# Attention and a ternary feed-forward layer on one core: Wo centred on chip, the variance behind Wo from ScalarE's sums of squares

## The chip, the cores and the metric

The kernel runs on one core of a Trainium2 chip. The metric is the device time of one execution in microseconds (us), as the median of several runs. The engines are named as the profile names them: PE is TensorE's matrix multiplication and PEld its loading of weights, DVE is VectorE, ACT is ScalarE, POOL is GpSimd, and SP is the engine that issues the DMAs. L818 is line 818 of the kernel before.

## The reference

The input x has 8 sequences of 1,024 tokens of width 256, in f32. Two sublayers follow one another, each with a LayerNorm (without weights) in front and one behind:

```python
x = x + _layernorm(attn(_layernorm(x), Wq, Wk, Wv, Wo))
x = x + _layernorm(ffn(_layernorm(x), weight, alpha, bias))
```

`attn` has 16 query heads of width 16 and 4 key and value heads, with a rotary embedding on queries and keys, a softmax over all 1,024 keys, and the product with Wo (256 x 256) at its end. `ffn` is one product with the ternary form (-1, 0, 1) of a 256 x 256 weight, times alpha, plus bias. `_layernorm` takes off the mean of the 256 elements and divides by the root of the variance plus 1e-5. What matters here is the LayerNorm behind Wo: its input is a = o @ Wo, and the first residual sum is x1 = x + layernorm(a).

## The kernel before

**Tiling.** The 8,192 tokens are cut into 16 units of 512 tokens, two to a sequence. For each unit a *project* part makes normalised tokens, queries, keys and values; 32 *steps* of attention follow (4 groups of heads by 8 blocks of 128 keys); then a *tail* divides by the softmax's sums, multiplies by Wo, and does everything up to the output. A tail has two *pairs* of two token tiles each (a tile is 128 tokens on the partitions by 256). The last tail (`LastTail`) has four parts of one tile each.

**A step.** TensorE computes scores twice: `sm` (L600), from which VectorE takes the row maxima (`mx`, L625), for a block of work ahead of time; and `se` (L673) with the maximum already taken off through extra rows of the queries, of which ScalarE makes the exponentials `e` (L694), 128x512 each. The product with the values, `av` (L714), follows two windows behind; a window is two or three of the four `se` of a step. TensorE's queue alternates `se` and `sm`. PSUM holds three banks in a ring for `se` and for most other products (pools `ps_e`, tag "se"), two double banks for `sm` (`ps_mx`), and one for `av`. A product in the ring waits until ScalarE has read the one three places before it.

**The order.** The instruction order on PE, DVE and ACT is written out by hand in program order, all through; POOL's order, outside the start and the end, and SP's order are chosen by a scheduler at build time. The lists `P_PARTS` and `T_PARTS` say in which of a unit's steps each part of a project and of a tail is issued; the tail of unit u runs beside the attention of unit u + 1 and the project of a later unit. `P_SECOND`, `T_FIRST`, `W_PARTS` and `T_LAST` shift these steps at the start and in the tails of units 12 to 14.

**The tail around Wo.** `attn(p)` multiplies by Wo into `pa` (L301, three products of high and low halves) and copies it to `a` on ScalarE (L818), at step 12 for pair 0 and step 15 for pair 1. `stats_a(p)`, at steps 15 and 17, runs `ln_stats`: on VectorE two BATCH_NORM_STATS2 (`bnst`, L237) and two aggregates (`mv`, L239); on GpSimd three small instructions (L241 to L243) that give minus the mean and 1 / sqrt(variance + eps). `add(p)` then normalises on GpSimd (L253, one instruction per tile, add and multiply) into `x1` and adds the residual `xr` (L823). `stats_x(p)`, from step 19, is the next LayerNorm, with VectorE's statistics of `x1`. The final LayerNorm (`stats_f`) is like it.

**Wo itself** is prepared once, in step 9 (`prepare_wo`): eight DMAs (L960) bring it in, and GpSimd splits it into a high part `woh` (L157) and a low part `wol` (L162).

Other names in the prediction: `xt` and `pt_xt` are transposed activations (L271, L267), `pkv` and `pq` the products for keys with values and for queries (L301), `kv_t` and `q_rot` their copies (L376, L457), `avsb` the copy of a finished `av` (L727), `d_k`, `k_rot` and `t2k` the way of the keys through DRAM and their rotation, `ml` the low part of the maxima that a DMA writes into the queries' extra rows `q_st` (L664), `part` a sum for the ternary threshold (L203).

Of the kernel before, what the change touches and what calls it, by code (L numbers as in the profile page):

```python
# [8 lines left out]
F32 = mybir.dt.float32  # L9
F32R = mybir.dt.float32r  # L10
AF = mybir.ActivationFunctionType
ALU = mybir.AluOpType
AX = mybir.AxisListType
# [3 lines left out]
P = 128  # L17
# [6 lines left out]
EPS = 1e-5  # L24
# [4 lines left out]
def kernel(  # L29
# [29 lines left out]
    nc = tc.nc  # L59
    B, S, D = x.shape  # L60
# [3 lines left out]
    ND = D // P  # L64
# [10 lines left out]
    small = ctx.enter_context(tc.tile_pool(name="small", bufs=4))  # L75
    work = ctx.enter_context(tc.tile_pool(name="work", bufs=2))
# [9 lines left out]
    def load_x(u, tag, bufs):  # L86
        b, half = divmod(u, UPB)
        t = xp.tile([P, UT, D], F32, tag=tag, name=f"{tag}_{u}", bufs=bufs)
        src = x[b, half * UQ : (half + 1) * UQ, :].rearrange("(t p) d -> p t d", p=P)
        for ts in (slice(0, 2), slice(2, 4)) if u == 0 else (slice(0, 4),):  # L90
            nc.sync.dma_start(out=t[:, ts, :], in_=src[:, ts, :])
        return t
# [6 lines left out]
    mhalf = const.tile([P, 2], F32, name="mhalf")  # L99
# [64 lines left out]
    def split(eng, hi, lo, src, hi_eng=None):  # L164

        split_hi(hi_eng or eng, hi, src)
        split_lo(eng, lo, src, hi)


    def parts_of(w, name):  # L170
        return [const.tile(list(w.shape), F32R, name=name + l) for l in "hl"]
# [11 lines left out]
    def psum(shape, name, dtype=F32):  # L183
        if spare[0]:
            spare[0] += 1
            if spare[0] % 5 < 2:
                return ps_mx.tile(shape, dtype, tag="sm", name=name)
        return ps_e.tile(shape, dtype, tag="se", name=name)
# [42 lines left out]
    def ln_stats(src):  # L231

        n = src.shape[1]
        mv = small.tile([P, 2, 2], F32, tag="mv", name="mv")[:, :n]
        st = small.tile([P, 2, 6], F32, tag="bnst", name="bnst")
        for t in range(n):
            nc.vector.bn_stats(st[:, t, :], src[:, t, :])  # L237
        for t in range(n):
            nc.vector.bn_aggr(mv[:, t, :], st[:, t, :])  # L239
        sc = small.tile([P, 2, 2], F32, tag="lnsc", name="lnsc")[:, :, :n]  # L240
        nc.gpsimd.tensor_scalar(sc[:, 1, :], mv[:, :, 1], EPS, 1.0, ALU.add, ALU.mult)  # L241
        nc.gpsimd.tensor_tensor(sc[:, 1, :], sc[:, 1, :], mhalf[:, :n], ALU.pow)  # L242
        nc.gpsimd.tensor_scalar(sc[:, 0, :], mv[:, :, 0], -1.0, 0.0, ALU.mult, ALU.add)  # L243
        return mv, sc
# [52 lines left out]
    def product(out, left, right, terms=TERMS):  # L297

        steps = [(i, j, c) for i, j in terms for c in range(ND)]
        for k, (i, j, c) in enumerate(steps):  # L300
            nc.tensor.matmul(  # L301
                out,
                chunk(left[i], c),
                chunk(right[j], c),
                start=(k == 0),
                stop=(k == len(steps) - 1),
            )
# [15 lines left out]
    class Project:  # L323
# [3 lines left out]
        def __init__(self, u, eng):  # L327
            self.u, self.eng = u, eng
            self.b, self.half = divmod(u, UPB)
            self.xt, self.sc, self.hl = {}, {}, {}  # L330
            self.q_rot = None
            if u not in (1, 2):
                xn = qkp.tile([P, UT, D], F32, tag="xn", name=f"xn_{u}", bufs=2)
                xs = qkp.tile([P, 2, UT, D], F32R, tag="hl", name=f"xs_{u}")
                self.xn = [xn[:, 2 * p : 2 * p + 2, :] for p in range(2)]
                self.xs = [[xs[:, l, 2 * p : 2 * p + 2, :] for l in range(2)] for p in range(2)]
            else:
                self.xn = [
                    tailp.tile([P, 2, D], F32, tag=f"xn{p}", name=f"xn_{u}_{p}") for p in range(2)
                ]  # L340
                self.xs = [
                    [ep.tile([P, 2, D], F32R, tag="e", name=f"xs_{u}_{p}_{l}") for l in range(2)]
                    for p in range(2)
                ]
# [393 lines left out]
    class Tail:  # L738
# [4 lines left out]
        def __init__(self, u):  # L743
            self.u = u
            self.xr = load_x(u, "xr", 1)
            self.a, self.on, self.hl, self.xt, self.x1, self.sc = {}, {}, {}, {}, {}, {}

        def new(self, what, p):
            shape, dtype = ([P, 2, 2, D], F32R) if what == "hl" else ([P, 2, D], F32)
            return tailp.tile(shape, dtype, tag=f"{what}{p}", name=f"{what}_{self.u}_{p}")  # L750
# [62 lines left out]
        def attn(self, p):  # L813
            pa = psum([P, self.width, D], f"pa_{self.u}_{p}")
            for t in range(self.width):
                product(pa[:, t, :], self.heads(self.width * p + t), wo_s)
            self.a[p] = self.new("a", p)
            self.copy(p)(self.a[p], pa)  # L818

        def add(self, p):  # L820
            x1 = self.x1[p] = self.new("x1", p)
# [5 lines left out]
            ln_apply(self.eng(p), self.on[p], self.x1[p], self.sc[p])  # L827

        def stats_a(self, p):
            self.sc[p] = ln_stats(self.a[p])  # L830
            self.add(p)

# [123 lines left out]
    def prepare_wo():  # L956
        wo = tailp.tile([P, ND, D], F32, tag="xn1", name="wo")
        rows = w_o.rearrange("(r c h d) n -> h r d c n", r=HKV, c=2, h=2)
        for i in range(2 * HKV):
            nc.sync.dma_start(out=wo[HD * i : HD * (i + 1)], in_=rows[i // HKV, i % HKV])  # L960
        wo_s.extend(parts_of(wo, "wo"))
        split(nc.gpsimd, *wo_s, wo)

# [97 lines left out]
    for u in range(3, NU):  # L1061
        start = SPU * (u - 4)
        steps = P_FIRST if u == 3 else P_SECOND if u == 4 else [k for k, *_ in P_PARTS]
        at(start + steps[0] - 6, load, u)
        if u == 3:
            for k, stage in (
                (7, measure), (9, prepare_wo), (11, add_up), (13, threshold), (15, ternarize),
                (22, transpose_ternary),
            ):
                at(k, stage)  # L1070
        at(start + steps[0] - 1, begin_project, u)
        for k, (_, *p) in zip(steps, P_PARTS):
            behind = [behind_latest] if u > 4 and p[0] in ("kt", "q_to_dram") else []
            at(start + k, *behind, part, projects, u, *p)
# [254 lines left out]
```

## Time and profile before

| What | Value |
|---|---|
| median of 3 runs | 1624.39 us (1623.93 to 1625.12) |
| span of the profiled execution | 1625.2 us |
| granted TensorE clock, mean | 0.997 |
| PE busy | 1576.5 us, 97% |
| PEld busy | 813.9 us, 50% |
| DVE busy | 1397.1 us, 86% |
| ACT busy | 1270.1 us, 78% |
| POOL busy | 833.8 us, 51% |
| `bnst` of `a` (both LayerNorms that read `a`), DVE | 120 instructions, mean 413 ns |
| `mv` (all LayerNorms), DVE | 256 instructions, mean 174 ns |
| `a<-pa` copy, ACT | 30 instructions, mean 585 ns |
| `e`, ACT | 1,996 instructions, mean 603 ns |

The span runs from the first to the last instruction of one execution, taken by the hardware profiler; the median is of runs timed from outside, and here lies 0.8 us below that span. In the profile's lines the first time is the start in us from the beginning of the span, the second the time for which the group was busy; a number in brackets is how long the engine stood idle just before, and the name behind the arrow is what it then waited for. The *chain of work that ended last* is found by going back from the last instruction, at each step to what released it; its shares say which engine's work the time consists of. The ends of matrix products are modelled, so a busy PE need not be a PE at its peak.

### The profile page before, as it was taken

The numbers are of one execution on the slowest core, as the hardware profiler recorded it, in microseconds if no ns is written. First come the engines' busy times: TensorE is split into PE (matmuls) and PEld (weight loads), VectorE is DVE, ScalarE is ACT, GpSimd is POOL, SyncE is SP. The second block draws the span as 40 slices with busy tenths as digits, with TensorE's granted clock in tenths as the row PEclk, the third lists the DMA queues.
The fourth block names the chain that finished last, engine by engine and source line by source line (L and its number), as shares of the span: only waits on it lengthen the run. The fifth ranks groups of instructions, "written<-read, shape, count | busy, mean of one in ns | idle before, by whom it ended". The sixth has DMA issues, their size and how long they took to land.

```text
span 1625.2 us, 37184 instructions
## 1 busy us (share of the span) xinstructions
PE 1576.5 (97%) x14702; PEld 813.9 (50%) x14702; DVE 1397.1 (86%) x2046; ACT 1270.1 (78%) x2473; POOL 833.8 (51%) x1239
## 2 busy tenths in 40 slices
PE   8999999999999999999999999999999999999997
PEld 6544454454545545454554545455454554444444
DVE  7878888889898888989889898988989888999964
ACT  4667878778787887878788787887878787787774
POOL 5542365364744637455364845546474552333354
PEclk9999999999999999999999999999999999999999
DMA  4151525124151422514133151513314141131100
GB/s 140 53 88 46 113 70 96 57 77 99 57 109 47 102 63 59 120 57 97 59 83 77 57 128 39 105 54 83 79 57 97 46 107 45 42 75 34 43 15 27
DMA packets 86078, 117.98 MB, mean 73 GB/s; under 512 B 12088, under 2 KB 50808, under 8 KB 85752
## 3 DMA queue, kind: packets, MB, share of 16 engines
q1 hardware_dynamic: 85904, 115.60, 29.7%
q8 instruction: 116, 1.90, 0.5%
q14 instruction: 58, 0.48, 0.1%
HBM read 68.65 MB, written 45.88 MB: 70 GB/s over the span
## 4 chain that ended last, share of the span: by engine, by line
PE 81%; DVE 10%; POOL 3%; ACT 2%; issue 2%; DMA 1%; SPq 0%; POOLq 0%; ACTq 0%; DVEq 0%
PE av L714 29%; PE se L673 28%; PE sm L600 9%; DVE mx L625 8%; PE pa L301 3%; PE pq L301 3%; PE pf L301 2%; ACT e L694 2%; PE pt_xt L267 2%; PE pt_ot L267 1%; PE pkv L301 1%; PE pm L648 1%; DVE bnst L237 1%; POOL lnsc L242 0%; DMA x<-in_L_attn_x 0%
## 5 line engine op out<-in xcount | busy, mean ns | idle before, releaser
L625 DVE TENSOR_REDUCE mx<-sm 128x2 f32<-128x1024 f32 (+1 forms) x1301 | 1204.8, 975 | 183.6 <-PE sm L600 164.0
L694 ACT ACTIVATE e<-se 128x512 f32<-128x512 f32 x1996 | 1057.0, 603 | 220.9 <-PE sm L600 163.7
L600 PE MATMUL sm<-k_st,q_st 64*128 64x512 f32 x2048 | 746.5, 448 | 7.2 <-DVE mx L625 4.1
L673 PE MATMUL se<-q_st,k_st 64*128 64x512 f32 x2048 | 705.6, 441 | 18.4 <-ACT e L694 14.6
L714 PE MATMUL av<-e,v_aug 128*32 128x256 f32 (+3 forms) x8584 | 606.0, 378 | 0.0
L673 PEld LDWEIGHTS se<-q_st,k_st 64*128 64x128 f32 x2048 | 324.5, 184 | 396.6 <-ACT e L694 305.4
L600 PEld LDWEIGHTS sm<-k_st,q_st 64*128 64x128 f32 x2048 | 325.2, 184 | 66.4 <-DVE mx L625 44.9
L714 PEld LDWEIGHTS av<-e,v_aug 128*32 128x32 f32 x8584 | 193.5, 108 | 212.5 <-issue 148.9
L241 POOL TENSOR_SCALAR lnsc<-mv 128x2 f32<-128x2 f32 (+1 forms) x134 | 26.1, 195 | 333.1 <-DVE mv L239 326.6
L788 POOL TENSOR_TENSOR xn<-xn,a 128x512 f32<-128x512 f32 x30 | 38.4, 1282 | 135.3 <-DMA a<-d_rec 130.0
L242 POOL TENSOR_TENSOR lnsc<-lnsc,mhalf 128x2 f32<-128x2 f32 (+1 forms) x134 | 92.5, 690 | 0.9
L157 POOL TENSOR_SCALAR xs<-xn 128x512 fp32r<-128x512 f32 x27 | 16.8, 621 | 130.8 <-DMA dq<-hlq 129.5
L162 POOL TENSOR_TENSOR hl<-xn,hl 128x512 fp32r<-128x512 f32 x54 | 68.7, 1285 | 0.1
L253 POOL TENSOR_SCALAR xn<-x,lnsc 128x256 f32<-128x256 f32 x116 | 64.3, 562 | 2.3
L853 POOL TENSOR_TENSOR a<-a,bias_bc 128x512 f32<-128x512 f32 x30 | 38.4, 1279 | 51.9 <-ACT a L852 51.9
L301 PE MATMUL pa<-woh,hl 128*128 128x256 f32 x240 | 46.2, 294 | 1.1 <-ACT e L694 1.1
L237 DVE BATCH_NORM_STATS2 bnst<-x 128x6 f32<-128x256 f32 x124 | 46.0, 413 | 1.3 <-DMA x<-in_L_attn_x 1.3
L315 POOL TENSOR_TENSOR t<-q_rot,sin_q_sb 128x512 f32<-128x512 f32 x31 | 39.7, 1282 | 12.2 <-ACT q_rot L457 12.1
L237 DVE BATCH_NORM_STATS2 bnst<-a 128x6 f32<-128x256 f32 x120 | 44.5, 413 | 0.0
L301 PE MATMUL pq<-xt,wqkvh 128*128 128x256 f32 x256 | 44.1, 294 | 0.5 <-ACT e L694 0.5
L457 ACT COPY q_rot<-pq 128x512 f32<-128x512 f32 x32 | 18.7, 586 | 28.3 <-PE pq L301 28.3
L301 PEld LDWEIGHTS pa<-woh,hl 128*128 128x128 f32 x240 | 34.6, 189 | 12.1 <-issue 6.3
(164 smaller groups left out, 1333.0 us busy)
## 6 DMA issues: line engine op xcount, KB each, us to landing
q_st<-dq SPq DMA_DIRECT2D x90, 256.0 KB
dq<-hlq SPq DMA_DIRECT2D x60, 256.0 KB
d_av<-avsb SPq DMA_DIRECT2D x60, 256.0 KB
x<-in_L_attn_x SPq DMA_DIRECT2D x15, 512.0 KB
xn<-d_av SPq DMA_DIRECT2D x30, 256.0 KB
a<-d_rec SPq DMA_DIRECT2D x30, 256.0 KB
xr<-in_L_attn_x SPq DMA_DIRECT2D x15, 512.0 KB
out_x<-a SPq DMA_DIRECT2D x30, 256.0 KB
```

Source lines behind the costliest of these rows:

```text
L162: eng.tensor_tensor(lo, src, hi.bitcast(F32), ALU.subtract)
L237: nc.vector.bn_stats(st[:, t, :], src[:, t, :])
L242: nc.gpsimd.tensor_tensor(sc[:, 1, :], sc[:, 1, :], mhalf[:, :n], ALU.pow)
L253: eng.tensor_scalar(dst[:, t, :], src[:, t, :], sc[:, 0, t : t + 1] if eng is nc.gpsimd else mv[:, t, 0:1], sc[:, 1, t : t + 1], ALU.add i ...
L267: nc.tensor.transpose(pt[:, c, t * P : (t + 1) * P], src[:, t, c * P : (c + 1) * P], ident_r)
L301: nc.tensor.matmul(out, chunk(left[i], c), chunk(right[j], c), start=(k == 0), stop=(k == len(steps) - 1),)
L315: eng.tensor_tensor(dst, x, table.unsqueeze(1).to_broadcast(list(x.shape)), ALU.mult)
L600: scores = nc.tensor.matmul(sm[0][:, part, :], queries[rows], k_st[(u // UPB) % 3][rows, r2, ch * 512 : (ch + 1) * 512], start=True, stop= ...
L625: early[0] = nc.vector.tensor_reduce(mx[i][:, a, head_and_tile(i, r2, t), lo:n], sm[0][:, lo:n, :], AX.X, ALU.max).ins
L673: nc.tensor.matmul(sc if len(queries.shape) == 2 else sc.rearrange("p (j t) -> p j t", j=G), k_st[(i // G // UPB) % 3][rows, r2, kt * P : ...
L694: nc.scalar.activation(e, sc, AF.Exp, scale=1.0 / D**0.5)
L714: nc.tensor.matmul(av_ps[0][32 * r : 32 * r + 32, lo:hi], va[:, kt, r, :], es[i * NK + kt, r // 2, r % 2][:, lo:hi], start=(kt == 0 and lo ...
```

## The change

Wo's rows are centred once: for each row of Wo its mean over the 256 columns is taken off, by one reduction on VectorE and three instructions on GpSimd. The mean of a row of a = o @ Wo is then zero, so that the variance is the mean of the squares. In all tails but the last, `attn` therefore adds two ScalarE instructions behind the copy of `pa`: Square over each tile, whose output goes to a scratch tile and whose row sum goes to `sq`. `stats_a` no longer calls `ln_stats` there but `add_scaled`: on GpSimd it turns `sq` into 1 / sqrt(sq / 256 + eps) with two small instructions, multiplies each tile by it (one instruction per tile, as before), and adds `xr`. The last tail keeps its statistics. The instructions of the other two LayerNorms stay as they were.

```diff
@@ class Tail, __init__
             self.a, self.on, self.hl, self.xt, self.x1, self.sc = {}, {}, {}, {}, {}, {}
+            self.sq = {}
@@ class Tail, attn
-            self.a[p] = self.new("a", p)
-            self.copy(p)(self.a[p], pa)
+            a = self.a[p] = self.new("a", p)
+            self.copy(p)(a, pa)
+            if self.width == 1:
+                return
+            sq = self.sq[p] = small.tile([P, 2], F32, tag="sq", name=f"sq_{self.u}_{p}")
+            junk = work.tile([P, D], F32, tag="sqj", name=f"sqj_{self.u}_{p}", bufs=1)
+            for t in range(self.width):
+                nc.scalar.activation(junk, a[:, t, :], AF.Square, accum_out=sq[:, t : t + 1])
+
+        def add_scaled(self, p):
+            x1, sq = self.new("x1", p), self.sq[p]
+            nc.gpsimd.tensor_scalar(sq, sq, 1.0 / D, EPS, ALU.mult, ALU.add)
+            nc.gpsimd.tensor_tensor(sq, sq, mhalf, ALU.pow)
+            self.x1[p] = x1
+            for t in range(self.width):
+                nc.gpsimd.tensor_scalar(
+                    x1[:, t, :], self.a[p][:, t, :], sq[:, t : t + 1], 0.0, ALU.mult, ALU.add
+                )
+            nc.gpsimd.tensor_tensor(x1, x1, self.xr[:, self.tiles(p), :], ALU.add)
@@ class Tail, stats_a
+            if self.width == 2:
+                self.add_scaled(p)
+                return
             self.sc[p] = ln_stats(self.a[p])
             self.add(p)
@@ prepare_wo, behind the DMAs
+        mean = small.tile([P, ND], F32, tag="wom", name="wom", bufs=1)
+        nc.vector.tensor_reduce(mean, wo, AX.X, ALU.add)
+        nc.gpsimd.tensor_scalar(mean, mean, -1.0 / D, 0.0, ALU.mult, ALU.add)
+        for c in range(ND):
+            nc.gpsimd.tensor_scalar(wo[:, c, :], wo[:, c, :], mean[:, c : c + 1], None, ALU.add)
         wo_s.extend(parts_of(wo, "wo"))
         split(nc.gpsimd, *wo_s, wo)
```

## The prediction, as it was put on record

> **What bounds the kernel now.** I read the clock first (0.997 granted over the span, so throttling is no part of this), then the chain of work that ended last, then busy time in equal stretches, then the engines' timelines around the code that changes.
>
> ```profile
> PE 81%; DVE 10%; POOL 3%; ACT 2%; issue 2%; DMA 1%; SPq 0%; POOLq 0%; ACTq 0%; DVEq 0%
> ```
>
> TensorE carries 81% of the chain. The stretches show a period: a unit's 32 steps repeat in 96.3 us.
>
> ```profile
> core 0: us, PE busy (x) PEld busy (x) DVE busy (x) ACT busy (x) POOL busy (x), PEclk, DMA share, GB/s
> 557.50:653.80 96.30, 94.83 (x920) 48.73 (x916) 85.13 (x125) 78.21 (x153) 53.24 (x78) 1.00 0.31 79
> ...
> 750.30:846.60 96.30, 94.81 (x922) 48.73 (x918) 85.15 (x124) 78.19 (x153) 53.24 (x78) 1.00 0.32 79
> ```
>
> By busy time, moving work from VectorE (DVE, 85 of 96 us) to ScalarE (ACT, 78) looks right. But what counts is who is late at the places where the work stands. Both places in one period, ScalarE's timeline (start, us, what, idle before):
>
> ```profile
> 596.18 0.58 ACT L818 COPY a<-pa 128x512 f32<-128x512 f32 x1 [0.82 <-issue]
> 597.14 1.09 ACT L694 ACTIVATE e<-se 128x512 f32<-128x512 f32 x2 [0.37 <-PE se L673]
> 598.11 0.59 ACT L271 CAST xt<-pt_xt 128x512 fp32r<-128x512 f32 x1
> 598.83 3.05 ACT L694 ACTIVATE e<-se 128x512 f32<-128x512 f32 x6
> 602.14 1.09 ACT L694 ACTIVATE e<-se 128x512 f32<-128x512 f32 x2 [0.27 <-PE sm L600]
> ```
>
> ```profile
> 604.04 0.58 ACT L818 COPY a<-pa 128x512 f32<-128x512 f32 x1 [0.81 <-issue]
> 605.21 1.58 ACT L694 ACTIVATE e<-se 128x512 f32<-128x512 f32 x3 [0.58 <-PE sm L600]
> 606.66 0.61 ACT L727 COPY avsb<-av 128x512 f32<-128x512 f32 x1
> 607.13 2.60 ACT L694 ACTIVATE e<-se 128x512 f32<-128x512 f32 x5
> 610.54 0.58 ACT L376 COPY kv_t<-pkv 128x512 f32<-128x512 f32 x1 [0.81 <-PE pkv L301]
> ```
>
> After each copy of pa ScalarE idles 0.37 or 0.58 us and is then packed for 4 to 5 us. The squares go into those gaps. VectorE's timeline at the statistics that disappear:
>
> ```profile
> 603.70 0.74 DVE L237 BATCH_NORM_STATS2 bnst<-a 128x6 f32<-128x256 f32 x2
> 604.36 0.30 DVE L239 BATCH_NORM_AGGREGATE mv<-bnst 128x2 f32<-128x6 f32 x2
> 605.48 4.68 DVE L625 TENSOR_REDUCE mx<-sm 128x2 f32<-128x1024 f32 x5 [0.82 <-PE sm L600]
> 610.08 0.74 DVE L237 BATCH_NORM_STATS2 bnst<-a 128x6 f32<-128x256 f32 x2
> 610.74 0.30 DVE L239 BATCH_NORM_AGGREGATE mv<-bnst 128x2 f32<-128x6 f32 x2
> 612.02 1.23 DVE L625 TENSOR_REDUCE mx<-sm 128x2 f32<-128x1024 f32 x1 [0.98 <-PE sm L600]
> ```
>
> Both are followed by VectorE waiting 0.82 and 0.98 us for TensorE: they hold nobody up.
>
> **Removed from VectorE.** 30 times two BATCH_NORM_STATS2 and two aggregates, 0.96 us from 603.70 to 604.66, 29 us in all. In the 11 regular tails (u = 1 to 11) and the first they are covered twice as above: gain 0. I looked behind all 30. Only three sit in a packed stretch that TensorE's sm then waits for: pair 1 of u = 12 and 13 (sm at 1381.32 and 1382.45 are late by 0.29 and 0.17 us, so 0.46 each) and pair 0 of u = 14 (sm at 1550.55 comes 0.7 later than its se at 1549.50 would let it). Gain 1.6 us in all.
>
> **Added to ScalarE.** The instruction order of the built program shows two squares behind each of the 30 copies, and otherwise ScalarE's, TensorE's and VectorE's orders as before. Each square waits for ScalarE's own instruction before it. The price of such a wait is in the start-up rows: L250 at 44.43 is followed by the dependent L251 at 44.98, 0.033 us after its end, where independent instructions overlap by about 0.11 (e takes 0.60 and repeats every 0.49). A square is 128x256 from SBUF to SBUF; the nearest row is L804's cast, 0.405 us (L390's copy from PSUM 0.382, L250's ACTIVATE with a bias per partition 0.505). The row sum that a square also delivers has no row in this trace. Call its cost r. It is bounded by 0 (folded into the square) and by 0.28 (the 244 ns of L650, ScalarE's smallest frequent instruction, plus the 0.033 wait); nearest is L210, one element per partition: 0.166 to 0.171 us long, and two of them start 0.067 apart. I take r = 0.12, between those two.
>
> Time added between the copy and the next e: copy with a dependent follower 0.585 + 0.033, less the 0.48 it costs now: 0.14; first square 0.405 + 0.033 + r; second 0.405 - 0.11 + r. Together A = 0.87 + 2r = 1.11 us.
>
> **From A to TensorE, pair 0.** Idle there: 597.14 - 596.18 - 0.48 = 0.48, so the e's run 0.63 late. The gap before 598.83 gives back 0.12. TensorE's se run in three banks, so each waits for the e three back in that ring: the one at 600.46 waits for an e that ends at 600.40 and would start near 600.9. But sm, its neighbour in TensorE's queue, starts at 600.72 anyway, because it waits for VectorE's maximum; this cover is worth 0.26. Late: 0.63 - 0.12 - 0.26 = 0.25 us. Without that cover it would be 0.51.
>
> **Pair 1.** Idle: 605.21 - 604.04 - 0.48 = 0.69, so 0.42 late, and packed up to 609.7. The key and value product pkv (608.80) takes the bank of the e that ends at 608.75: slack 0.02. Late: 0.40 us. Behind pkv ScalarE (0.81) and VectorE idle, so TensorE never gets it back.
>
> **Sum.** A regular tail: 0.65 us, times 11: 7.2. Tail u = 0: pair 0 about 0.3, pair 1 nothing (0.77 us of idle time before its kv_t copy). Tails 12 and 13: gap 0.58 at both pairs; 0.26 at pair 0, pair 1 hidden behind VectorE's waits, less 0.46: -0.4 for both. Tail 14: +0.25 - 0.7 = -0.45. Once, near 95.8 us, the reduction of wo (128x512, nearest row L203, 0.677) enters a packed VectorE stretch and moves the sm at 97.61: +0.6. Its DMAs landed by 60.9, when woh is made now, so it waits for none. Total 7.2 + 0.3 - 0.4 - 0.45 + 0.6 = **+7.25 us**.
>
> **At nothing.** *GpSimd* loses one 0.19 us instruction per pair, and sq is ready about 6 us before mv is now, so x1 is early; stats_x is not waiting for it now (bnst<-x idles 1.3 us in all, for DMAs). The three centring steps (0.2 + 2 x 0.55) and woh, wol now fall near 97 to 101 us, beside the split of the third unit's queries (97.42, 98.12), whose readers come at step 33 (170 us); woh is first read at 213. *SP*: in the built order the 512 KB load of xr moves ahead of the d_k store and the k_rot loads. It waits for x1 of pair 1 (sq near 606, then some 3.4 us of GpSimd: 609.4); d_k is issued at 611.15, so the queue isn't held. If it were, the t2k step would be late (it waits 35.5 us for k_rot in all already), which is not on the chain. In tail 14 xr moves ahead of the shift's q_st<-ml pair (1553.33); x1 is done near 1550.4, so 3 us remain. The four-buffer pool small gains sq and loses one use each of mv, bnst and lnsc; I count no wait from it.
>
> [...] Per 256 elements VectorE pays 0.413 + 0.174 for mean and variance, and ScalarE's cast row 0.405 for one pass. [...]
>
> **Rivals.** (1) *The row sum is free* (r = 0): A = 0.87, pair 0 late 0.01, pair 1 0.16; 11 x 0.17 = 1.9, + 0.1 - 0.9 - 0.7 + 0.6 = +1.0: **1625.4**. For it: ScalarE idles 18 of 96 us. Against: the short instruction rows. (2) *Dear squares*: 0.505 as in L250 and r = 0.2 (L210 with its wait): A = 1.47, late 0.61 + 0.76; 11 x 1.37 = 15.1, the rest +1.5: **1641**. (3) *VectorE's relief reaches TensorE, faster*: if at most of the 30 places, as at u = 12, 0.5 us of TensorE's wait hangs on the statistics, and ScalarE's gaps take the squares whole (A at most 0.5): -15 + 0.6: **1610**. It decides where VectorE has no idle time before its next mx. For it: 10% of the chain is VectorE's; against: the 0.82 and 0.98. (4) *It doesn't do what it says*: Square needs another function table. One ACT_TABLE_LOAD is 1.283 us; two per pair are 60, 77 us: **1702**. The built order has a single load, as now.
>
> **Numbers.** The profiled span 1625.2 is 0.8 above the median of the runs, 1624.39, so I add to the median: 1624.4 + 7.25 = **1631.6**. Chances: forecast 0.55, rival 1 0.18, rival 2 0.17, rival 3 0.08, rival 4 0.02. Ends: r = 0 gives 1625.4; r = 0.28 gives A = 1.43, late 0.57 + 0.72, 1640; range 1625.4 to 1639.5, which leaves out rivals 3 and 4 and part of 2. Within 0.2% (3.2 us, about what a measurement of this kernel tells from no change) lies rival 1; forecast, 2 and 4 are slower: 0.74, 0.18 and 0.08.
>
> **What would show it.** The period becomes 96.95; squares of 0.4 us with a short row behind each; the 0.37 and 0.58 before e gone at both copies; pkv and the se before it late by 0.4; VectorE's idle time after 603.70 up by the whole 0.96. Wrong if a square takes 0.6 or more, or if the period shrinks: then VectorE was late where I read TensorE as late.

## The result and the profile after

The changed kernel takes 1636.14 us (1634.05 to 1639.39 in 4 runs) beside 1624.64 us for the kernel before on the same chip: a ratio of 1.0071, interval 1.0056 to 1.0086. It is 11.5 us slower. The forecast was 1631.6 (7.25 us slower) with a range of 1625.4 to 1639.5. The span of the profiled execution is 1637.6 us.

The chain of work that ended last, in the changed kernel:

```profile
PE 83%; DVE 8%; ACT 3%; DMA 2%; POOL 2%; issue 1%; SPq 0%; POOLq 0%; DVEq 0%; ACTq 0%
```

VectorE's share falls from 10% to 8%, and TensorE's, ScalarE's and the DMAs' shares rise. Whether TensorE waited for the work taken off VectorE the shares alone do not tell; experiment e2 does. Busy time in one regular period (the 32 steps of unit 7, which was 96.30 us):

```profile
core 0: us, PE busy (x) PEld busy (x) DVE busy (x) ACT busy (x) POOL busy (x), PEclk, DMA share, GB/s
757.74:854.77 97.03, 95.53 (x920) 48.66 (x916) 83.47 (x116) 80.04 (x161) 52.72 (x76) 1.00 0.33 78
```

VectorE has 1.7 us less to do, ScalarE 1.8 us more, and the period is 0.73 us longer at full clock. ScalarE's timeline at the copy of pair 0 (start, us, what, idle before), which answers to the first one of before:

```profile
602.07 0.59 ACT L819 COPY a<-pa 128x512 f32<-128x512 f32 x1 [0.82 <-issue]
602.69 0.42 ACT L825 ACTIVATE sqj<-a 128x256 f32<-128x256 f32 x1
603.01 0.18 ACT L825 ACTIVATION_READ_ACCUMULATOR sqj<-a 128x1 f32 x1
603.23 0.42 ACT L825 ACTIVATE sqj<-a 128x256 f32<-128x256 f32 x1
603.55 0.19 ACT L825 ACTIVATION_READ_ACCUMULATOR sqj<-a 128x1 f32 x1
603.64 1.06 ACT L694 ACTIVATE e<-se 128x512 f32<-128x512 f32 x2
```

Each row sum is a short instruction of its own behind its square. The idle 0.37 us ahead of `e` is gone, and `e` starts 1.57 us after the copy instead of 0.96. VectorE at the same place:

```profile
605.33 1.22 DVE L625 TENSOR_REDUCE mx<-sm 128x2 f32<-128x1024 f32 x1 [0.82 <-PE sm L600]
```

This is the second maximum behind the copy; it follows the copy's start by 3.26 us. In the kernel before it was 2.92 (599.10 after 596.18):

```profile
599.10 3.55 DVE L625 TENSOR_REDUCE mx<-sm 128x2 f32<-128x1024 f32 x4 [0.47 <-PE sm L600]
```

VectorE, too, is later, because the `sm` that it reads stands behind the late `se` in TensorE's queue. At pair 1 the squares push `e` from 1.17 to 1.57 us behind the copy, and VectorE's idle time behind the vanished statistics grows to 1.70 us:

```profile
611.71 3.55 DVE L625 TENSOR_REDUCE mx<-sm 128x2 f32<-128x1024 f32 x4 [1.70 <-PE sm L600]
```

To see where the 12.4 us between the two profiled spans lie, I cut both traces at the first `se` of every unit. Period n is the attention of unit n; the tail of unit n - 1 runs in it. Period 15 is counted up to the first `se` of its last step, and the end from there on.

| Stretch | before, us | after, us | difference |
|---|---|---|---|
| up to the first `se` | 59.95 | 59.70 | -0.25 |
| period 0 | 110.48 | 110.87 | +0.39 |
| period 1 (tail 0) | 98.16 | 101.45 | +3.28 |
| periods 2 to 12 (tails 1 to 11, "regular") | 1059.50 | 1067.86 | +8.36 |
| periods 13, 14, 15 (tails 12 to 14) | 90.56, 91.41, 90.94 | 90.26, 91.17, 91.12 | -0.36 |
| behind the last step | 24.21 | 25.17 | +0.97 |

Two thirds are the forecast mechanism. Two items were not forecast, most of period 1 and the end. Of period 1's 3.28 us, 0.68 are at its step 10, which scatters without the change too (-0.44 us in a second profile of the kernel before); 0.44 are at steps 16 and 17, where the squares of tail 0 stand; 2.17 are at steps 23 to 25. In period 1 TensorE waits for the DMA that brings the shift into the queries (`q_st<-ml`). It already did so in the kernel before:

```profile
244.00 0.46 PE L673 MATMUL se<-q_st,k_st 64*128 64x512 f32 x1 [1.26 <-DMA q_st<-ml]
```

The changed kernel, that wait, and the clock behind it:

```profile
246.16 0.47 PE L673 MATMUL se<-q_st,k_st 64*128 64x512 f32 x1 [2.13 <-DMA q_st<-ml]
```

```profile
246.00:248.00 2.00, 1.84 (x14) 0.70 (x14) 1.07 (x1) 1.34 (x3) 1.95 (x2) 0.85 0.06 12
248.00:250.00 2.00, 2.00 (x14) 1.02 (x14) 1.54 (x4) 1.23 (x4) 1.88 (x4) 0.50 0.41 121
```

The wait is 0.87 us longer, and behind it the granted clock (PEclk, third number from the end) falls to 0.50; in the kernel before it stayed at 1.00. At the end of the program the same shows: a pause of 1.78 us (1.75 before), and only in the changed kernel the clock then falls to 0.50. Why the `q_st` DMA is late is seen in SP's queue (start, us, DMA) and in GpSimd's first product of the keys' rotation, `t2k`, which waits for the `k_rot` loads. The changed kernel's first:

```profile
225.85 0.50 SPq L431 DMA_DIRECT2D d_k<-kv_t  x1
227.42 0.39 SPq L91 DMA_DIRECT2D xr<-in_L_attn_x  x1
228.13 1.20 SPq L435 DMA_DIRECT2D k_rot<-d_k  x2
```

```profile
232.82 0.74 POOL L315 TENSOR_TENSOR t2k<-k_rot,sin_kt_sb 128x256 f32<-128x256 f32 x1 [5.43 <-DMA k_rot<-d_k]
```

Then the kernel before:

```profile
224.56 0.49 SPq L431 DMA_DIRECT2D d_k<-kv_t  x1
226.82 1.20 SPq L435 DMA_DIRECT2D k_rot<-d_k  x2
229.13 0.39 SPq L91 DMA_DIRECT2D xr<-in_L_attn_x  x1
```

```profile
230.78 0.73 POOL L315 TENSOR_TENSOR t2k<-k_rot,sin_kt_sb 128x256 f32<-128x256 f32 x1 [1.67 <-DMA k_rot<-d_k]
```

In the changed kernel the load of `xr` (512 KB) stands ahead of the `k_rot` loads and is held until GpSimd has finished `x1` (226.10 + 1.29 = 227.39). The `k_rot` loads are not issued later for it: they follow the store `d_k` by 2.28 us here and by 2.26 before. They land later: `t2k` starts 4.69 us after their issue here and 3.96 before. The rotation of the keys, its stores and loads, and the `q_st<-ml` pair behind them in the queue, all move with it.

### The profile page after: what moved, and what is told of

The parts are those of the page before. It is cut to its first block, busy times and chain, and to the rows that moved or that the text cites. A ratio compares the mean times of both kernels' runs of the same rounds, so it can differ in the third digit from the quotient of the medians.

```text
span 1637.6 us, 37119 instructions
## 1 busy us (share of the span) xinstructions
PE 1587.8 (97%) x14702; PEld 815.1 (50%) x14702; DVE 1373.7 (84%) x1927; ACT 1297.6 (79%) x2593; POOL 828.7 (51%) x1212
## 4 chain that ended last, share of the span: by engine, by line
PE 83%; DVE 8%; ACT 3%; DMA 2%; POOL 2%; issue 1%; SPq 0%; POOLq 0%; DVEq 0%; ACTq 0%
PE se L673 30%; PE av L714 30%; PE sm L600 9%; DVE mx L625 7%; PE pa L301 3%; PE pq L301 3%; PE pf L301 2%; ACT e L694 2%; PE pt_xt L267 2%; PE pt_ot L267 1%; PE pkv L301 1%; PE pm L648 1%; DMA d_av<-avsb 1%; DVE bnst L237 0%; POOL lnsc L242 0%
## 5 line engine op out<-in xcount | busy, mean ns | idle before, releaser
L600 PE MATMUL sm<-k_st,q_st 64*128 64x512 f32 x2048 | 756.2, 451 | 7.1 <-DVE mx L625 4.3
L673 PE MATMUL se<-q_st,k_st 64*128 64x512 f32 x2048 | 716.2, 443 | 20.1 <-ACT e L694 14.9
L241 POOL TENSOR_SCALAR lnsc<-mv 128x2 f32<-128x2 f32 (+1 forms) x104 | 20.5, 197 | 159.3 <-DVE mv L239 153.0
L829 POOL TENSOR_SCALAR sq<-sq 128x2 f32<-128x2 f32 x30 | 5.8, 193 | 138.6 <-ACT sqj L825 138.6
L242 POOL TENSOR_TENSOR lnsc<-lnsc,mhalf 128x2 f32<-128x2 f32 (+1 forms) x104 | 71.8, 691 | 0.9
L315 POOL TENSOR_TENSOR t2k<-k_rot,sin_kt_sb 128x256 f32<-128x256 f32 x14 | 10.3, 734 | 114.0 <-DMA k_rot<-d_k 114.0
```

Source lines behind the costliest of these rows:

```text
L315: eng.tensor_tensor(dst, x, table.unsqueeze(1).to_broadcast(list(x.shape)), ALU.mult)
L600: scores = nc.tensor.matmul(sm[0][:, part, :], queries[rows], k_st[(u // UPB) % 3][rows, r2, ch * 512 : (ch + 1) * 512], start=True, stop= ...
L673: nc.tensor.matmul(sc if len(queries.shape) == 2 else sc.rearrange("p (j t) -> p j t", j=G), k_st[(i // G // UPB) % 3][rows, r2, kt * P : ...
```

## The experiments

**Theory A**: the squares stand between ScalarE's copy of `pa` and the next `e`; TensorE's ring waits for that `e`, and VectorE's relief reaches nobody. **Theory B**: the load of `xr`, moved ahead in SP's queue, disturbs the transfers in every period. **Theory C**: the centred Wo, ready later by three GpSimd steps, holds up the first periods. **Theory D**: VectorE's relief does reach TensorE. **Theory E**: ScalarE as a whole is short of time. For period 1 and the end there was a question of its own: a wait that the change brings, or chance.

All times are medians beside the kernel before on the same chip, whose medians were 1625.54 (e1 to e4), 1625.66 (the repeats, e5, e6) and 1625.57 (e7, e8). On those chips its single runs lay between 1622 and 1641 us, so that the intervals are wide. The time goes with the mean granted clock that is recorded with each run (over the 78 runs of the kernel before: median 1623.5 us at 0.999 and 1.000, 1630.2 at 0.996 and less, and the slowest, 1641.0, at 0.987). The lengths of the regular periods, which repeat to some hundredths, tell more.

| Kernel | time, us | ratio to before (95%) | regular period (median) | period 1 (wait for `q_st<-ml`) | periods 13, 14, 15 | end |
|---|---|---|---|---|---|---|
| before | 1624.64 | 1 | 96.30 | 98.16 (1.26) | 90.56, 91.41, 90.94 | 24.21 |
| before_again | 1622.87, one run | | 96.33 | 97.47 (0.99) | 90.60, 91.44, 90.89 | 24.25 |
| after | 1636.14 | 1.0071 (1.0056 to 1.0086) | 97.04 | 101.45 (2.13) | 90.26, 91.17, 91.12 | 25.17 |
| after_again | 1635.26 | 1.0062 (1.0050 to 1.0074) | 97.03 | 100.32 (1.93) | 90.25, 91.19, 91.09 | 25.11 |
| e1_centre_only | 1625.24 | 0.9992 (0.9973 to 1.0010) | 96.27 | 99.94 (1.45) | 90.55, 91.46, 91.01 | 24.19 |
| e2_no_variance | 1627.45 | 1.0005 (0.9985 to 1.0024) | 96.32 | 101.37 (3.04) | 89.94, 90.80, 90.18 | 24.98 |
| e3_no_row_sum | 1632.62 | 1.0036 (1.0018 to 1.0054) | 96.65 | 101.61 (2.75) | 90.08, 90.98, 90.52 | 25.30 |
| e4_xr_behind | 1631.38 | 1.0029 (1.0008 to 1.0049) | 97.05 | 97.76 (none) | 90.25, 91.16, 91.07 | 24.20 |
| e5_gaps | 1627.90 | 1.0014 (1.0000 to 1.0028) | 96.29 | 96.93 (none) | 90.30, 91.18, 91.12 | 25.07 |
| e6_gaps_all | 1625.13 | 1.0003 (0.9991 to 1.0015) | 96.31 | 96.86 (none) | 89.95, 90.82, 91.08 | 25.22 |
| e7_warm | 1633.61 | 1.0044 (1.0027 to 1.0062) | 97.01 | 100.57 (3.04) | 90.29, 91.17, 91.10 | 24.23 |
| e8_best | 1622.72 | 0.9986 (0.9971 to 1.0002) | 96.33 | 97.61 (none) | 89.99, 90.88, 90.95 | 24.19 |

**e1_centre_only.** Wo's centring stays, the rest is undone:

```diff
-            sq = self.sq[p] = small.tile(...)
-            ... the two squares
         def stats_a(self, p):
-            if self.width == 2:
-                self.add_scaled(p)
-                return
             self.sc[p] = ln_stats(self.a[p])
```

> Only the centring of Wo's rows; the LayerNorm behind Wo keeps VectorE's statistics and ScalarE gets no squares. The lost time was counted as: 11 regular tails 8.35 us (96.30 to about 97.04 us a period), the period after the first tail 3.3, the end 1.0. Theory A (the squares stand between ScalarE's copy of pa and the next e, and TensorE's se waits for that e): the centring costs the one late sm near 97.6 us, +0.6 us or less; regular periods stay at 96.30; in all 0 to +1 us against before, ratio 1.0000 to 1.0006. Theory B (the load of xr, which moved ahead in SP's queue, disturbs the transfers in every period): the same, since xr stays where it was. Theory C (the centred wo, later by its three GpSimd steps, holds up the first periods): more than +1.5 us, all of it before 260 us.

Regular periods are as before, and no time difference is seen. Of theory C only the reduction is there: step 11 of period 0 takes 3.02 us instead of 2.44, and period 0 as a whole 109.31, beside 108.93 in before_again, both at full clock. Period 1 is 1.8 us longer here too, 1.6 of it at steps 23 to 25, although `xr` stands where it stood: the wait for `q_st<-ml` is 1.45 instead of 1.26 us, and behind it the clock fell to 0.50. So the wait is there in both profiles of the kernel before (1.26 and 0.99 us) and here, and behind the longest of the three alone the clock fell.

**e2_no_variance.** No squares; a constant takes the place of the row sums:

```diff
-                nc.scalar.activation(junk, a[:, t, :], AF.Square, accum_out=sq[:, t : t + 1])
...
-            nc.gpsimd.tensor_scalar(sq, sq, 1.0 / D, EPS, ALU.mult, ALU.add)
+            nc.gpsimd.tensor_scalar(sq, one2, 1.0 / D, EPS, ALU.mult, ALU.add)
```

> The changed kernel without its squares: the variance behind Wo is left out, a constant stands in its place, so VectorE's statistics are gone and ScalarE gets nothing; x1 is early and the load of xr moves ahead in SP's queue as in the changed kernel. Theory A: regular periods 96.30 (VectorE's relief reaches nobody), -1.6 us in the last tails, +0.6 for the centring, and in the period after the first tail the +2.2 us of the SP queue: +1 us in all, ratio 0.9990 to 1.0020. Theory B: every regular period stays long, 96.7 to 97.0, ratio 1.003 to 1.006. Theory D (VectorE's relief reaches TensorE): periods below 96.1, ratio below 0.998.

Regular periods are 96.32, with VectorE's statistics gone and `xr` ahead in the queue: theories B and D fall. Taking 1.8 us of work per period from an engine that is busy for 85 of 96 us gave nothing. The relief shows in periods 13 to 15 alone: -0.62, -0.62 and -0.76, 2.0 us in all. Period 1 and the end are long here too, so neither comes from the squares. In period 1 `xr` is issued ahead even of `d_k` here and in e3; `k_rot` then follows `d_k` by 3.8 to 3.9 us instead of 2.3, and the wait for `q_st<-ml` is the longest (3.04 and 2.75 us).

**e3_no_row_sum.** The squares run, without `accum_out`; `sq` comes from a constant as in e2.

> The changed kernel with its squares, but without their row sums (a constant stands in the variance's place), so that no accumulator is read: the squares' own price and that of the reads apart. Theory A with the reads as costly as their 187 ns rows less the overlap (0.10 to 0.15 each): the e behind the pa copy starts 0.2 to 0.3 us earlier than in the changed kernel, a regular period is 96.45 (96.35 to 96.65) instead of 97.04, and the time is 4 to 7 us below the changed kernel's, ratio to before 1.002 to 1.004 (the period after the first tail and the end still long). Theory A2 (the reads are hidden, the two squares alone do it): periods 96.9 to 97.05, ratio 1.006 to 1.007. Theory B: as A2, since xr is ahead in the queue here too.

Two squares alone cost 0.34 us a period, half of the whole: the reads are not hidden, nor are they the whole. ScalarE's timeline of this run at pair 0:

```profile
600.65 0.58 ACT L821 COPY a<-pa 128x512 f32<-128x512 f32 x1 [0.83 <-issue]
601.27 0.87 ACT L826 ACTIVATE sqj<-a 128x256 f32<-128x256 f32 x2
602.04 1.07 ACT L696 ACTIVATE e<-se 128x512 f32<-128x512 f32 x2
```

From copy to `e` it is 1.39 us, with the reads 1.57: a read of 187 ns costs 0.09 us of ScalarE's time here; it starts 0.32 us into a square of 0.42, and so runs partly beside its end. Two pairs of two reads are 0.36 us; the period grows by 0.39. With ScalarE's gap full here, all of the added time is found in the period.

**e4_xr_behind.** The whole change, with the load of `xr` put back behind the `k_rot` loads:

```diff
-            self.xr = load_x(u, "xr", 1)
+            if 0 < u < NU - 3:
+                with tc.issue_after(projects[u + 3].k_in):   # the last k_rot load
+                    self.xr = load_x(u, "xr", 1)
+            else:
+                self.xr = load_x(u, "xr", 1)
```

> The changed kernel whole, with the load of xr put back behind the k_rot loads in SP's queue, where it stood before. Theory A: regular periods stay at 97.0 (96.95 to 97.1); the period after the first tail loses the 2.2 us that TensorE waited there for q_st<-ml and the slow clock behind it, +0.7 to +1.2 instead of +3.3; in all 2 to 3 us below the changed kernel, ratio to before 1.0045 to 1.0062. Theory B: regular periods go back to 96.3 to 96.5 and the ratio to 1.0003 to 1.002. If the 2.2 us were a chance of one execution: no difference to the changed kernel, ratio 1.0065 to 1.008.

Regular periods stay at 97.05, so B falls a second time. Period 1 loses the wait entirely and the clock stays at 1.00 up to the last matmul. Two things do this. `t2k` starts 3.78 us after the issue of `k_rot`, as in the kernel before (3.96 and 3.65 in its two profiles). And GpSimd's order, which the scheduler chooses, is another one here: the keys' split `ks`, which their store waits for, comes ahead of the queries' product `t`, in the kernel before behind it.

```profile
230.95 0.40 POOL L157 TENSOR_SCALAR ks<-k_rot 128x256 fp32r<-128x256 f32 x1
231.32 1.27 POOL L315 TENSOR_TENSOR t<-q_rot,sin_q_sb 128x512 f32<-128x512 f32 x1
```

```profile
233.23 1.28 POOL L315 TENSOR_TENSOR t<-q_rot,sin_q_sb 128x512 f32<-128x512 f32 x1
234.47 0.41 POOL L157 TENSOR_SCALAR ks<-k_rot 128x256 fp32r<-128x256 f32 x1
```

From `t2k` to the keys' first store (`dk<-ks`) it is 3.02 us here, 4.14 before and 4.16 in the changed kernel. So of the 2.0 us by which the `q_st<-ml` pair comes earlier behind `d_k` than in the changed kernel, 0.9 belong to the place of `xr` and 1.1 to this order, and this run alone doesn't part what each saves in time. Each beside the kernel before on its chip, the time is 4 to 6 us below the changed kernel's, more than expected: I had not counted on the wait going to zero, nor on the clock at the end.

**before_again and after_again**, the two kernels once more.

> The kernel before once more, for its profile beside those of this call: regular periods 96.30, the first period 109 to 111 and TensorE's wait for q_st<-ml in the period after the first tail near 1.3 us. Two theories of the period after the first tail: if the granted clock falls there by the length of that wait, then it falls where the wait is 1.4 us or more (the run with the centring alone: 1.45 us, and the clock fell) and not where it is 1.26 or less; if by chance, there is no such order among the runs.

> The changed kernel once more, on the same chip as the two below. Theory A: regular periods 97.03 again (0.73 over before, of which the squares alone were 0.34 and the reads of their sums 0.39), the last three tails -0.4 us in all; the period after the first tail +3 with a wait for q_st<-ml over 2 us; ratio to before 1.005 to 1.0075. What the first period and the end of the program add (+0.4 and +1.0 in its first profile) should change from run to run if it is chance.

Regular periods repeat to 0.03 us, period 1 and the end repeat roughly. Over the first ten profiles the order by length holds in period 1: no pause, 0.99 and 1.26 us left the clock at 1.00; behind 1.45, 1.93, 2.13, 2.75 and 3.04 us it fell to 0.50 each time. At the end all ten pauses are 1.74 to 1.80 us long, and the clock fell behind six of them, where the end is 0.8 to 1.1 us longer: the length doesn't decide there, and what does was not shown. In both profiles of the changed kernel periods 4 and 5 are 0.2 to 0.3 us longer than the other regular ones (0.28 of it at step 14 of period 4); e4 and e7 do not have this, and its cause stays open.

**e5_gaps.** The same squares, at other places of ScalarE's order, in tails 1 to 11, with `xr` as in e4:

```diff
         def attn(self, p):
...
+            if p == 1:
+                do_squares()          # pair 0's, ahead of pair 1's copy
             a = self.a[p] = self.new("a", p)
             self.copy(p)(a, pa)
+            squares.append((self, p))
...
         def kv(self, p):
...
+                do_squares()          # pair 1's, ahead of the kv_t copy
                 nc.scalar.copy(self.kv_t, self.pkv)
```

> The changed kernel with the load of xr behind the k_rot loads, and in the 11 regular tails the squares moved to where ScalarE has nothing to do: those of pair 0 just ahead of pair 1's copy of pa, those of pair 1 just ahead of the kv_t copy (idle time of 0.81 us at both in the kernel before). Same instructions, same number. Theory A (what counts is that the squares stand between the copy and the next e): regular periods back to 96.30 to 96.45, in all -1 to +1 us against before, ratio 0.9993 to 1.001, 7 to 8 us below the kernel with xr behind alone. Theory E (ScalarE as a whole is short, so 2.2 us more per period cost the same wherever they stand): periods stay at 97.0, ratio 1.004 to 1.006.

The period is back to 96.29, as A says and E excludes. ScalarE, and busy time in one period (unit 7):

```profile
598.64 0.42 ACT L844 ACTIVATE sqj<-a 128x256 f32<-128x256 f32 x1
598.95 0.20 ACT L844 ACTIVATION_READ_ACCUMULATOR sqj<-a 128x1 f32 x1
599.18 0.42 ACT L844 ACTIVATE sqj<-a 128x256 f32<-128x256 f32 x1
599.50 0.19 ACT L844 ACTIVATION_READ_ACCUMULATOR sqj<-a 128x1 f32 x1
599.60 0.56 ACT L832 COPY a<-pa 128x512 f32<-128x512 f32 x1
600.74 0.60 ACT L701 ACTIVATE e<-se 128x512 f32<-128x512 f32 x1 [0.58 <-PE sm L607]
```

```profile
745.76:842.08 96.32, 94.84 (x922) 48.73 (x918) 83.39 (x116) 79.78 (x161) 52.78 (x76) 1.00 0.33 79
```

ScalarE is as busy as in the changed kernel (79.78 us, 161 instructions) and the 0.7 us are gone: the squares now lie where ScalarE idled 0.82 us while TensorE made `pa`, and the 0.58 us ahead of `e` are still there. The ratio of 1.0014 lies above the 0.9993 to 1.001 that I expected: its runs scatter from 1622.4 to 1634.2. Their granted clock goes with it: 0.998 to 1.000 in the four runs up to 1623.7, 0.996 and 0.997 in the four near 1628, 0.990 to 0.994 in the four above 1630. Where the high ones lose it no profile shows, since only a low one was profiled. One such place is the start-up: the first `se` comes at 57.7 to 58.7 us in the six profiles whose clock stays at 1.00 there, at 59.7 to 60.0 behind 3.4 us at 0.50, at 60.8 to 60.9 behind 6.8 us, and at 63.4 behind 10.2 us.

**e6_gaps_all.** Pair 0's squares of tails 12 to 14 are moved ahead of pair 1's copy as well.

> As the one before, and in the last three tails with statistics by squares (12 to 14) pair 0's squares too stand just ahead of pair 1's copy. Theory A: in these three periods the squares' and reads' price (0.3, 0.35 and 0.9 us by the run without variance against the changed kernel) goes at least by half, so that they are -0.5, -0.5 and -0.3 us against before instead of -0.3, -0.25 and +0.15; in all 0.5 to 1 us below the one before in the sum of periods, which is under what the times can tell; ratio 0.9988 to 1.0005. Theory E: no difference to the one before.

Periods 13 and 14 reach -0.61 and -0.59, all that e2 had shown to be there. Period 15 stays at +0.14. The reason is in VectorE's timeline of the changed kernel there:

```profile
1559.87 0.25 DVE L927 RECIPROCAL rec<-pos 128x16 f32<-128x16 f32 x1 [0.71 <-ACT pos L924]
1560.15 0.61 DVE L929 TENSOR_TENSOR xn_last<-pos,rec 128x256 f32<-128x256 f32 x1
```

The last tail has begun in this period. Pair 1's squares push ScalarE's copy `pos`, the reciprocal `rec` waits for it at the head of VectorE's queue (0.11 us in the kernel before, 0.71 here), and the next `mx` stands behind it (at 1560.69).

**e7_warm.** The changed kernel with 13 matmuls in the two pauses, into banks of the ring, with results that nobody reads:

```diff
-    WARM = {0: 12, 1: 6}
+    WARM = {0: 12, 1: 6, 7: 7}
...
                 if t == 3 and j == 2:
+                    self.fill(6)
```

> The changed kernel with 13 matmuls into a spare bank added: 7 where TensorE waits for q_st<-ml in the period after the first tail (pauses of 2.13 and 1.93 us in its two profiles), 6 between the two halves of the last transposes of the heads (pauses of 1.74 to 1.80 us in every profile; the granted clock fell to 0.50 behind them in 6 of 10). Theory (a pause of TensorE, and not the wait as such, brings the slow clock, and the slow clock costs about 1 us each time): the clock stays at 1.00 behind both places; the period after the first tail goes from +2.2 to +3.3 over before to +1.0 to +2.0 (the wait itself stays); the end goes from +0.9 to +1.0 back to 0 to +0.1; regular periods stay at 97.03; 1.5 to 2.5 us below the changed kernel, ratio to before 1.004 to 1.006. Rival (the clock falls for another reason, or the added matmuls only take the pause's place): no difference, 1.0055 to 1.0075.

The wait for `q_st<-ml` happened to be as long as in e2, so the two can be compared. TensorE at that place in e7 and in e2, and the clock in e2 behind it:

```profile
240.39 1.89 PE L692 MATMUL se<-k_st,ident_r 128*128 128x512 f32 x7
243.43 0.50 PE L673 MATMUL se<-q_st,k_st 64*128 64x512 f32 x1 [1.15 <-DMA q_st<-ml]
```

```profile
243.60 0.46 PE L675 MATMUL se<-q_st,k_st 64*128 64x512 f32 x1 [3.04 <-DMA q_st<-ml]
```

```profile
244.00:246.00 2.00, 2.00 (x14) 0.51 (x10) 1.63 (x2) 1.61 (x3) 1.83 (x4) 0.56 0.24 32
246.00:248.00 2.00, 2.00 (x18) 0.99 (x14) 1.12 (x3) 1.12 (x3) 2.00 (x3) 0.58 0.28 108
```

Both wait 3.04 us from the end of their work to the data. In e7 1.89 us of it are filled, the pause is 1.15, the clock stays at 1.00 up to the last matmul, and steps 23 to 25 take 1.73 us more than in the kernel before. In e2, unfilled, they take 3.06 more. So the longer wait is 1.73 of it (3.04 - 1.26 = 1.78), and the slow clock 1.3 us. By the same sum the changed kernel's steps 23 to 25 come out: 0.87 + 1.3 = 2.17, measured 2.17. The end is 24.23 instead of 25.1 to 25.2. In period 1 the gain did not show in full, since the wait itself was longer this time.

**e8_best.** e6, pair 1's squares of tail 14 at its `stats_a`, and 6 matmuls in the last pause.

> The version to which the experiments point: squares in ScalarE's gaps in all tails from the second on, the load of xr behind the k_rot loads, in tail 14 pair 1's squares later, with its stats_a (in the changed kernel they delay ScalarE's pos copy, for which VectorE's rec and through it the next mx wait: rec idle 0.71 us), and 6 matmuls in the last pause. Expected by period: regular 96.30; the one after the first tail 96.9; the last three -0.6, -0.6 and -0.6 (was +0.14) against before; the end 24.2 instead of 25.2; behind the first period 2.5 to 4 us below before, ratio 0.9975 to 0.9990. Rival for tail 14 (the removal there is lost whatever the place): +0.1 in that period.

Regular periods and periods 13 and 14 came as expected. Period 1 took 97.61 us instead of 96.9; most of this is at its steps 6 to 8 and 10, which vary from profile to profile. The profiled execution started late (first `se` at 63.39 us); behind period 0 it is 1.2 to 1.5 us shorter than the two of before, instead of 2.5 to 4. The rival for tail 14 won: period 15 is +0.01. `pos` and `rec` are back in their places (37.10 and 37.73 us into the period, 37.10 and 37.72 in the kernel before). But `xn_last`, which takes 0.42 us in the kernel before and 0.61 in the changed one, takes 1.08, beside GpSimd's addition of `x1` (1.29 us from 1548.44; `xn_last` from 1548.93), so that step 13 gives back 0.20 of e2's 0.77; and pair 1's squares at their new place lengthen step 15 by 0.26.

The interval, 0.9971 to 1.0002, does not quite exclude no change. Part of the lower median is clock: 9 of the 12 runs had 0.999 or 1.000 granted, of the 20 runs of the kernel before 6. Among these the medians are 1622.61 and 1623.08, half a microsecond apart. So with ScalarE's squares in its gaps the change brought 0.5 to 1.5 us of 1625 here.

## Why the prediction was right, and where it was wrong

**Right: the mechanism and the sign.** VectorE's removed 29 us gave nothing in the regular tails (e2: 96.32), the squares cost at the copies (e3, e5), and the price per pair was near the forecast: A, the time added between copy and `e`, was 1.11 us; it is 1.09 (1.57 less the 0.48 that the copy costs anyway). The share r of a row sum was taken as 0.12; it is 0.09, an instruction of its own. The squares without it make 0.91, forecast 0.87.

**Mis-sized: the regular tail**, 0.65 forecast, 0.72 measured (the mean without periods 4 and 5), so 7.9 in place of 7.2 for 11, plus the 0.5 of periods 4 and 5 that stays open. Pair 1's 0.40 came as 0.37. Pair 0's 0.25 came as 0.34, and the term that failed is the cover of 0.26: "sm, its neighbour in TensorE's queue, starts at 600.72 anyway, because it waits for VectorE's maximum". The maximum does not stay where it was: its own `sm` stands in the queue behind the `se` that is now late, so `mx` comes 0.34 us later (3.26 instead of 2.92 us behind the copy). Of the cover 0.14 was left (step 14 +0.48, step 15 -0.14 in unit 7).

**Wrong: the new place of `xr` put at nothing.** The reason given was "the queue isn't held", worked out for a regular tail. Held it isn't, even in tail 0, where `xr` waits for `x1` until 227.42: `k_rot` follows `d_k` by 2.28 us there, by 2.26 in the kernel before. What the reason leaves out is the transfer itself: with the 512 KB of `xr` issued 0.71 us ahead of them the `k_rot` loads land 0.6 to 1.1 us later (`t2k` starts 6.83 to 6.97 us behind `d_k` in the three profiles with this order, 5.90 to 6.22 in the three with the old one; 6.06 in e4). In the regular tails this costs nothing (e2, e4). In tail 0, whose steps stand elsewhere (`T_FIRST`, `P_SECOND`), this way is on the path: TensorE waits for `q_st<-ml` at its end. I looked at one tail and took it for all. Beside the first profile of the kernel before, it cost 0.9 us in one profile and 0.7 in the other by the wait alone.

**Not thought of: the clock.** "Throttling is no part of this" was nearly true of the trace of before (up to its last matmul its clock fell twice, for 3.4 us each, in the start-up and in period 0) and not of the changed kernel: behind pauses of 2.13 and 1.93 us in period 1 its clock fell to 0.50 for 3.4 us, by the sum under e7 1.3 us lost, and it fell at the end, which is 0.9 to 1.0 us longer, in both of its profiles.

**The small terms.** Tail 0: +0.3 forecast for pair 0, +0.44 measured (steps 16 and 17); pair 1 cost nothing, as forecast (step 18: 3.65 us before, 3.63 after; ScalarE's idle time ahead of `kv_t` falls from 0.77 to 0.36). Tails 12 and 13: -0.4 forecast, -0.54; pair 0 cost 0.38 in each instead of 0.26, and the relief was 0.66 instead of 0.46. Tail 14: -0.45 forecast, +0.14 to +0.18: the gain of 0.76 is there (e2), but pair 1's squares, which I counted at nothing, reach VectorE through `pos` and `rec`. The reduction of Wo: +0.6 forecast, +0.59 measured: step 11 of period 0 takes 2.44 us in the two profiles without centring and 3.02 to 3.03 in all ten with it. (Period 0 as a whole scatters by 1.5 us: 110.48 and 110.87 us in the first profiles of both kernels, in which the clock fell to 0.50 in it for 3.4 us, 108.93 and 109.31 in before_again and e1 at full clock.)

**The sum.** 7.9 + 0.5 (regular), 0.4 + 0.8 + 1.3 (tail 0, wait, clock), 0.6 (Wo) and -0.4 (last tails) make 11.1; the end adds 0.9 where the clock falls. Measured: 11.5 and 9.6 us in the two comparisons of medians, whose runs differ in granted clock. That this lies inside the range is in part luck: the range was made wide for the price r of a row sum, which came out near its forecast, and what filled it are terms put at nothing and a clock not thought of.

**The rivals.** VectorE's relief (3) and table loads (4) are excluded, the latter by the single table load of 1.283 us in the profile. A free row sum (1) would have been e3's 96.65 us a period, not the 96.47 I gave it, for the same failed cover. A square of 0.505 us (2) did not come: it takes 0.418.

## What to carry to other kernels

Before moving work to an engine with idle time, ask where in its order the work will stand: the same squares cost 0.73 us a period behind a copy that the next exponential follows, and nothing 7 us later ahead of a copy that waits for TensorE anyway. A cover counts only if the thing that covers does not itself wait for what becomes late. A DMA moved in its queue has to be followed in each kind of period, the first above all, for what it delays in transfer as much as for what it holds (in the changed kernel's tail 0 the `k_rot` loads were not issued later and landed 0.6 to 1.1 us later). A pause of TensorE should be counted with the clock behind it: five pauses of 1.45 to 3.04 us in period 1 were followed by a clock of 0.50 for 3.4 us, which in e2 cost 1.3 us beside a wait longer by 1.8.

## What the runs showed of the hardware

- A row sum on ScalarE is an ACTIVATION_READ_ACCUMULATOR of 187 ns behind its ACTIVATE of 418 ns (60 of each), and lengthens the sequence by 0.09 us: from the copy to the next `e` it is 1.57 us with two of them and 1.39 without (e3).
- In period 1 the granted clock fell to 0.50 for 3.4 us behind TensorE's pauses of 1.45, 1.93, 2.13, 2.75 and 3.04 us (e1, after_again, after, e3, e2), 0 to 2 us after work had begun again; behind 0.99, 1.15 and 1.26 us (before_again, e7, before) it stayed at 1.00. At the end it fell behind six of ten pauses of 1.74 to 1.80 us (1.78 in the changed kernel, where it fell, 1.75 in the kernel before, where it did not). In period 0 it fell in the first profiles of both kernels behind a pause of 1.00 us, and not in the ten others, which have this pause too. So the length of the pause alone does not say when the clock falls; what does was not shown.
- VectorE's `xn_last` (128x256) took 0.42 us in the kernel before, with no GpSimd work beside it, 0.43 in e2, with 0.15 us of GpSimd's addition of `x1` beside its start, 0.61 in the changed kernel, beside 0.35 us of GpSimd's scaling of a tile and 0.17 us of that addition, and 1.08 in e8, beside 0.80 us of it. This was seen, not tested by itself.
